# A planned decoder layer: the first two sequences' order, the split of sequences in the front, and the first row scaling

## The chip, the cores and the metric

The kernel runs on one core of a Trainium2 chip. The metric is device time in microseconds (us) of one execution, the median over runs. The profile is one execution of its own; its span runs from the first to the last instruction.

Engine names in the profile: PE is TensorE (matmuls), PEld its weight loads, DVE is VectorE, ACT is ScalarE, POOL is GpSimd, SP is SyncE, which issues nearly all DMAs. A "q" behind a name (SPq, ACTq) marks what an engine's queue issues, DMAs above all.

## The reference

Sixteen sequences of 512 tokens and 256 channels go through one decoder layer in float32, with a layer norm after each of three blocks:

```python
x = _layernorm(x + attn(x))           # long convolution block and a gated MLP
x = _layernorm(x + xattn(x, ctx))     # causal self attention + cross attention, 16 heads of 16
x = _layernorm(x + ffn(x))            # low rank MLP
# attn:  z = rmsnorm(u) @ in_proj.T ; z = short_conv(z) ; x2, x1, v = split(z)
#        xv = x1*v ; y = (long_conv(xv, h) + xv*D_skip) * x2 ; y = y @ out_proj.T + u
#        return y + gelu(rmsnorm(y) @ l1.T) * (rmsnorm(y) @ l2.T) @ l3.T
```

h is a sum of 16 decaying exponentials for each channel. x2 is called the gate below.

## The kernel before

The program has two stages. Each is a list of operations with a cost, a priority (smaller goes first), the tiles that it reads and writes, and the engines that may run it. `Plan.schedule` (L103) places them greedily by these costs, gives every operation a buffer of its class's pool, and emits the instructions in the order found; each engine then runs its own list strictly in order and waits by semaphores. The order is therefore fixed when the program is built, and a wait at the head of an engine's list holds everything behind it.

**The front** (L372 to L987) computes the long convolution of all sequences at once. For each sequence b, `prepare` (L446) loads x, takes the row norms (L319), scales on GpSimd (L333) and transposes (L348). `x1v(b, k)` (L508) projects x1 and v for channel half k (two matmul pairs at L485, short convolution on ACT L492 and DVE L500, product on GpSimd L512), transposes (L518) and copies into `xv[k]`. `gate_of` (L529) projects the two halves of the gate and stores them to DRAM, by SP at L541, or by ACT at L535 for those that are held until after the last matmul of the convolution (`far_done`, L762). The convolution itself is eight blocks, four for each channel half. A block has four Toeplitz tiles of 512 KB ("toes") that SP loads from `hpad` (L669) into the x slots and GpSimd masks (L679), matmuls at L694 (near), L745 (toes) and L757 (far), and four results copied (L301 or L299) and stored to `yconv` (L776).

Three numbers at L432 say how sequences are split in the front. The last LATE sequences do only `x1v(b, 0)` at first, and `x1v(b, 1)` and their gates later, between or beside the blocks. The last KEPT of these hold their normalised x in SBUF (three in the tiles `early`, two in x slots); the other late ones store it to DRAM (`normed`, L557) and load it again (L568). The last LAST sequences project their gates after `far_done`. There are seven x slots, and waiting toes use the same slots.

At the end of the front x, gate and yconv half 0 of sequence 0 are loaded into the three `early` tiles (L792).

**The second stage** (from L1033) runs for each sequence `first_block` (L1107: load y and gate, product L1135, output projection L1148, add L1094, row norm L319/L308/L309, `x_ += y1` on GpSimd L1160, scaling L335, transposes L348, MLP L1173, L1203, L1225, layer norm L1046/L1067), `attention` (L1237: transposes L348, projections L1326 and L1254, context keys L1278 and values L1303, score maxima L1421, scores L1543 with exponentials on ACT L1513, sums L1573, cross attention L1601/L1621, output L1083) and `ffn` (L1732). Sequence b's first block is planned beside the attention of sequence b-1, whose waits for ACT it fills. Its output projection waits (`after`) for the list `begun`, the transposes of that attention's input (L1153, L1241); the context matmuls L1278 and L1296 wait for it too. There is one buffer for y, one for the gate, one for y1, and three PSUM buffers `mm`, besides one `scores` (four banks) and one `av`.

`scale_ops` (L327) scales the four row groups of a tile; for y1 all four run on ACT (L1163).

Of the kernel before, what the change touches and what calls it, by code (L numbers as in the profile page):

```python
# [197 lines left out]
def decoder_layer(  # L198
# [39 lines left out]
    B, T, D = x.shape  # L238
# [46 lines left out]
    def dve(n):  # L285
        return 0.16 + n / 960.0

    def act(n, bias=False):
        return 0.18 + n / 1200.0 + (0.12 if bias else 0.0)

    def pool_(n):
        return 0.2 + n / 470.0
# [20 lines left out]
    def rms_ops(x, prio):  # L313

        sq, junk = Buf("small"), Buf("junk")
        for c in range(NT):
            plan.op(
                "ACT", act(D) + 0.2,
                lambda e, c=c: nc.scalar.activation(  # L319
                    junk.t, x.t[:, c, :], AF.Square, accum_out=sq.t[:, c, 0:1]  # L320
                ),
                prio, r=[(x, c)], w=[(sq, c), junk],
            )
        rsqrt_op(sq, 0, 1.0 / D, 1e-6, prio)
        return sq

    def scale_ops(x, sq, prio, on):  # L327
        for c in range(NT):

            def fn(e, c=c):  # L330
                if e != "ACT":
                    eng = nc.vector if e == "DVE" else nc.gpsimd
                    eng.tensor_scalar(x.t[:, c, :], x.t[:, c, :], sq.t[:, c, 8:9], None, ALU.mult)  # L333
                else:
                    nc.scalar.activation(x.t[:, c, :], x.t[:, c, :], AF.Copy, scale=sq.t[:, c, 8:9])  # L335

            cost = {"POOL": pool_(D), "DVE": dve(D), "ACT": act(D, True)}[on]
            plan.op(on, cost, fn, prio, r=[sq], w=[(x, c)])

    def transposed(src, view, prio, dst=None):  # L340

        dst = dst or Buf("xT")
        for k in range(KD):
            ps = Buf("mm")

            def tr(e, k=k, ps=ps):
                for c in range(NT):
                    nc.tensor.transpose(ps.t[:, bass.ts(c, P)], view(src.t)[:, c, bass.ts(k, P)], ident)  # L348

            plan.op("PE", TR, tr, prio, r=[src], w=[ps])  # L350
            plan.op(
                "ACT DVE", (act(T), dve(T)), lambda e, k=k, ps=ps: copy(e, dst.t[:, k, :], ps.t), prio,
                r=[ps], w=[(dst, k)],
            )
        return dst
# [16 lines left out]
    with ExitStack() as front:  # L372
# [56 lines left out]
        marks = []  # L429


        LATE, KEPT, LAST = 9, 5, 2  # L432

        def at_step(n):
            return marks[n : n + 1] if n >= 0 else ()
# [6 lines left out]
        def as_xT(b):  # L442
            n = b - (B - KEPT)
            return View(f"e{n}" if 0 <= n < 3 else "x", lambda t: t.rearrange("p (k n) -> p k n", k=KD))

        def prepare(b, pr):  # L446

            x_ = View("x", lambda t: t.rearrange("p (c d) -> p c d", c=NT))
            for c in range(0, NT, 1 if b == 0 else NT):
                cs = slice(c, c + (1 if b == 0 else NT))  # L450
                plan.op(
                    "SP", 0.5 if b == 0 else 0.5 * MB,
                    lambda e, cs=cs: nc.sync.dma_start(
                        out=x_.t[:, cs, :], in_=x[b].rearrange("(c p) d -> p c d", p=P)[:, cs, :]
                    ),
                    pr - 1000, w=[(x_, c)] if b == 0 else [x_], lat=2.5, after=at_step(b - 3),
                )
            if b == 0:
                load_in(prew, pre_w, -900, [(INW, "p")])
                for k in range(KD):  # L460
                    load_in(inw[:, k, :], in_wT[bass.ts(k, P), :], -900, [(INW, k)])
                load_in(cw, conv_w, -890, [(CW, 0)])
                load_in(cb, conv_b, -890, [(CW, 1)])
                for k in range(KD):
                    plan.op(
                        "DVE", 0.9,
                        lambda e, k=k: nc.vector.tensor_scalar(
                            inw[:, k, :], inw[:, k, :], prew[:, k : k + 1], None, ALU.mult
                        ),
                        -900, r=[(INW, "p")], w=[(INW, k)],  # L470
                    )

            sq = rms_ops(x_, pr - 120)
            scale_ops(x_, sq, pr - 120, "POOL" if b else "DVE")
            xT = transposed(x_, lambda t: t, pr - 120, as_xT(b))
            marks.append(plan.ops[-1])
            return xT
# [69 lines left out]
        for b in range(B):  # L547
            xT = prepare(b, b * 100)
# [4 lines left out]
            else:  # L553
                if b < B - KEPT:
                    plan.op(
                        "SP", 0.5 * MB,
                        lambda e, b=b, xT=xT: nc.sync.dma_start(  # L557
                            out=normed[b - B + LATE], in_=xT.t.rearrange("p k n -> p (k n)")
                        ),
# [3 lines left out]
        for b, xT in late:  # L563
            if b < B - KEPT:
                xT = as_xT(b)
                plan.op(
                    "SP", 0.5 * MB,
                    lambda e, b=b, xT=xT: nc.sync.dma_start(  # L568
                        out=xT.t.rearrange("p k n -> p (k n)"), in_=normed[b - B + LATE]
                    ),  # L570
# [85 lines left out]
        for blk in range(NR // R8):  # L656
# [106 lines left out]
            for c in range(HPG):  # L763
# [8 lines left out]
                for par in range(2):  # L772
# [9 lines left out]
                    o = plan.op("ACT" if par and blk >= NR // R8 - 3 else "SP", 0.6, store, pc + 10, r=[res], lat=3.0)  # L782
# [318 lines left out]
    def add_row(x, row, prio):  # L1101
        def fn(e):
            nc.gpsimd.tensor_tensor(x.t, x.t, row.unsqueeze(1).to_broadcast([P, NT, D]), ALU.add)

        plan.op("POOL", pool_(NT * D), fn, prio, w=[x])

    def first_block(b, after):  # L1107

        p0, p1, p2 = (b - 2) * 1000 + 300, (b - 1) * 1000 + 100, (b - 1) * 1000 + 150
# [30 lines left out]
        y1 = Buf("y1")  # L1140
# [14 lines left out]
        sq = rms_ops(y1, p0)  # L1155
        for cp in range(NT // 2):
# [3 lines left out]
                lambda e, sl=sl: nc.gpsimd.tensor_tensor(x_.t[:, sl, :], x_.t[:, sl, :], y1.t[:, sl, :], ALU.add),  # L1160
                p0, r=[(y1, 2 * cp), (y1, 2 * cp + 1), sq], w=[(x_, 2 * cp), (x_, 2 * cp + 1)],
            )
        scale_ops(y1, sq, p0, "ACT")  # L1163
        zT = transposed(y1, lambda t: t, p0)
        gT = Buf("gT")
        for f in range(NF):
# [70 lines left out]
    def attention(b, x_):  # L1237

        p0, p1, p3 = (b - 1) * 1000 + 600, b * 1000, (b + 1) * 1000 + 250
        xT = transposed(x_, lambda t: t, p0)  # L1240
        begun = [o for _, o, w in xT.seen if w]  # L1241
        add_row(x_, bias_p, p0 + 100)
        va, vc, yT = Buf("va"), Buf("vc"), Buf("xT")
        keys = [Buf("keys") for _ in range(G)]
# [27 lines left out]
        if b % 2 == 0:  # L1272
# [3 lines left out]
            def kc_mm(e, ps=ps):  # L1276
# [13 lines left out]
                p0, r=[ps], w=[kcs_of[-1]],  # L1290
# [523 lines left out]
    begun, held, kcs_of = (), [], []  # L1814
    for b in range(B):
        x_ = first_block(b, begun)
        begun = attention(b, x_)
        ffn(b, x_)
# [98 lines left out]
```

## Time and profile before

| what | value |
|---|---|
| median of 3 runs | 2086.71 us (2084.34, 2086.71, 2374.48) |
| the profiled execution: its own time | 2084.24 us |
| its span | 2082.2 us |
| what lies around the span | 2.0 us |
| PE busy | 2006.2 us, 96% of the span |
| DVE, ACT, POOL busy | 1329.4, 1029.3, 766.9 us |
| first matmul of the convolution blocks (L694) | 172.75 us |
| last matmul of the convolution (L757) ends | 264.2 us |
| first output projection (L1148) | 281.56 us |
| first transposes of the first attention (L348) | 333.24 us |
| first score maxima of the first and second attention (L1421) | 358.24 and 452.97 us |

In the timeline each row has the start, the busy time of a merged group, engine, line, operation, output and input, the number of instructions, and in brackets the idle time of the engine just before, with what ended it. In the table by windows the columns are the window, its length, busy time and number of instructions for each engine, then the granted PE clock (1.00 is full), the DMA engines' share and GB/s. A float32 matmul shows as two PE records.

### The profile page before, as it was taken

Reading aid. Unit: us, or ns where it says so; the run is one execution under the profiler, and the core shown is the slowest. Engines: PE = TensorE matmul, PEld = TensorE weight load, DVE = VectorE, ACT = ScalarE, POOL = GpSimd, SP = SyncE. Lnnn points to the kernel's source line nnn. Section 1 sums busy time; section 2 is a strip of 40 time slices with the busy share of each in tenths; the row PEclk is TensorE's granted clock in tenths of the full one; section 3 lists DMA queues with packets and bytes.
Section 4 is the critical chain, followed back from the end, with each engine's and each line's share of the span. In section 5 each row is a group of like instructions: output and inputs, shape, how many; then the busy total and the mean of one; then the engine's idle time right before and its main releaser. Section 6 shows DMA issues by size and latency. Waiting matters only on the chain. (4 is left out here: it accounts for less than half of the span.)

```text
span 2082.2 us, 36835 instructions
## 1 busy us (share of the span) xinstructions
PE 2006.2 (96%) x14900; PEld 1053.5 (51%) x14900; DVE 1329.4 (64%) x1920; ACT 1029.3 (49%) x1465; POOL 766.9 (37%) x1036
## 2 busy tenths in 40 slices
PE   7999978999999999999999999999999999999987
PEld 4455645555554545454545454454545454545443
DVE  7987533737584848484857576666767584656554
ACT  6864422656435262717161626253534446655773
POOL 7695612243323241414142424232323233533432
PEclk9999989999999999999999999999999999999999
DMA  6365861030304040413131312223131404031200
GB/s 195 110 212 184 273 214 51 6 119 17 119 11 144 12 134 22 123 33 117 38 108 48 100 56 88 68 70 85 56 100 33 123 13 129 18 101 45 71 22 31
DMA packets 114939, 182.22 MB, mean 88 GB/s; under 512 B 13393, under 2 KB 62034, under 8 KB 114642
## 3 DMA queue, kind: packets, MB, share of 16 engines
q1 hardware_dynamic: 113234, 177.26, 27.8%
q8 instruction: 117, 1.92, 0.4%
q10 hardware_dynamic: 1536, 2.62, 0.4%
q14 instruction: 52, 0.43, 0.1%
HBM read 111.09 MB, written 68.76 MB: 86 GB/s over the span
## 5 line engine op out<-in xcount | busy, mean ns | idle before, releaser
L1513 ACT ACTIVATE ex<-scores 128x2048 f32<-128x2048 f32 (+1 forms) x228 | 362.4, 1606 | 193.5 <-PE scores L1543 140.6
L1173 PE MATMUL mm<-xT,w_l 128*128 128x512 f32 x640 | 299.7, 609 | 0.0
L1560 POOL TENSOR_SCALAR_AFFINE_SELECT ex<-ex 128x512 f32<-128x512 f32 x256 | 158.6, 634 | 324.7 <-ACT ex L1513 323.2
L1421 PE MATMUL scores<-keys,q 32*128 32x192 f32 (+5 forms) x2848 | 225.3, 426 | 6.2 <-ACT ex L1444 4.6
L1543 PE MATMUL scores<-q,keys 32*128 32x256 f32 (+3 forms) x2240 | 183.3, 435 | 11.8 <-ACT ex L1513 10.9
L1421 PEld LDWEIGHTS scores<-keys,q 32*128 32x128 f32 x2848 | 123.8, 184 | 138.5 <-issue 41.1
L1772 ACT ACTIVATE row<-mm,b_s 128x512 f32<-128x512 f32 x124 | 78.9, 686 | 224.7 <-PE mm L1764 224.0
L1173 PEld LDWEIGHTS mm<-xT,w_l 128*128 128x128 f32 x640 | 114.6, 190 | 141.5 <-issue 134.3
L1703 POOL TENSOR_TENSOR nd<-nd,nd 128x1024 f32<-128x1024 f32 x30 | 70.7, 2357 | 299.9 <-DMA nd<-di 299.9
L1573 PE MATMUL av<-ex,va 128*32 128x512 f32 (+3 forms) x2048 | 164.8, 438 | 0.8 <-POOL ex L1560 0.8
L1225 PE MATMUL mm<-w_l,gT 128*128 128x256 f32 x640 | 160.7, 386 | 0.0
L308 POOL TENSOR_SCALAR small<-small 128x4 f32<-128x4 f32 (+1 forms) x66 | 13.2, 200 | 399.7 <-DVE small L1047 359.6
L500 DVE SCALAR_TENSOR_TENSOR frow<-fmm,cw,frow 128x511 f32<-128x511 f32 x192 | 141.0, 744 | 25.9 <-ACT frow L492 21.1
L1470 DVE TENSOR_TENSOR scores<-scores,mask_qk 128x1024 f32<-128x1024 f32 x132 | 115.6, 876 | 60.4 <-PE scores L1421 57.4
L1185 ACT ACTIVATE row<-mm 128x512 f32<-128x512 f32 x80 | 47.8, 598 | 209.6 <-PE mm L1173 209.6
L1543 PEld LDWEIGHTS scores<-q,keys 32*128 32x128 f32 x2240 | 96.9, 184 | 107.5 <-ACT ex L1513 67.3
L1444 ACT COPY ex<-scores 128x1024 f32<-128x1024 f32 (+1 forms) x96 | 114.3, 1228 | 65.7 <-PE scores L1421 53.0
L485 PE MATMUL fmm<-fx,inw 128*128 128x512 f32 x312 | 143.4, 604 | 0.0
L1225 PEld LDWEIGHTS mm<-w_l,gT 128*128 128x128 f32 x640 | 117.2, 190 | 44.6 <-issue 31.1
L299 DVE COPY row<-av 128x512 f32<-128x512 f32 x60 | 41.5, 691 | 134.9 <-PE av L1573 124.4
L1326 PE MATMUL mm<-xT,wqc_s 128*128 128x512 f32 x256 | 126.3, 611 | 0.0
L1332 DVE TENSOR_SCALAR q<-mm,bqc_s 128x512 f32<-128x512 f32 x62 | 46.6, 751 | 100.0 <-PE mm L1326 100.0
(210 smaller groups left out, 3485.9 us busy)
## 6 DMA issues: line engine op xcount, KB each, us to landing
dn<-row SPq DMA_DIRECT2D x120, 256.0 KB
keys<-dk SPq DMA_DIRECT2D x64, 256.0 KB
nd<-dn SPq DMA_DIRECT2D x30, 512.0 KB
nd<-di SPq DMA_DIRECT2D x30, 512.0 KB
fx<-hpad SPq DMA_DIRECT2D x28, 512.0 KB
early<-gates SPq DMA_DIRECT2D x16, 512.0 KB
early<-yconv SPq DMA_DIRECT2D x32, 256.0 KB
dk<-row SPq DMA_DIRECT2D x32, 256.0 KB
```

The lines of the kernel that those rows point to most:

```text
L485: nc.tensor.matmul(ps.t, inw[:, k, bass.ts(m, P)], xT.t[:, k, :], start=(k == 0), stop=(k == KD - 1))
L500: lambda e, lag=lag: nc.vector.scalar_tensor_tensor(t.t[:, lag:], ps.t[:, 0 : T - lag], cw[:, m, 2 - lag : 3 - lag], t.t[:, lag:], ALU.mul ...
L1173: nc.tensor.matmul(ps.t, w[:, k, bass.ts(f, P)], zT.t[:, k, :], start=(k == 0), stop=(k == KD - 1))
L1225: nc.tensor.matmul(ps.t[:, bass.ts(cc, D)], gT.t[:, f, bass.ts(c, P)] if f < NF else gE.t, w_l3[:, f, :] if f < NF else w_l3e[:, c, :], st ...
L1326: nc.tensor.matmul(ps.t, w[:, k, cols], xT.t[:, k, :], start=(k == 0), stop=(k == KD - 1))
L1421: nc.tensor.matmul(sc.t[:, r, lo:hi], q.t[hd, bass.ts(i, P)], kk.t[hd, k0 - at + lo : k0 - at + hi], start=True, stop=True,)
L1444: lambda e, sc=sc, both=both, cols=cols: nc.scalar.copy(both.t[:, :, cols], sc.t[:, :, cols]),
L1470: nc.vector.tensor_tensor(diag, diag, mask, ALU.add)
L1513: lambda e: nc.scalar.activation(ex.t.rearrange("p (r n) -> p r n", r=HPG)[:, :, cols], sc.t[:, :, cols], AF.Exp, scale=scale),
L1543: nc.tensor.matmul(sc.t[:, r, lo:hi], keys[g].t[hd, TC + j * P : TC + (j + 1) * P], qas[g].t[hd, q0 + lo : q0 + hi], start=True, stop=True,)
L1560: lambda e, ex=ex, at=at: nc.gpsimd.affine_select(out=ex.t.rearrange("p (r n) -> p r n", r=HPG)[:, :, at : at + P], in_=ex.t.rearrange("p ...
L1573: nc.tensor.matmul(av[g].t[bass.ts(r, SLOT), j * P :], va.t[:, j, h * VS : h * VS + SLOT], ex.t[:, r * T + at : r * T + at + n], start=(j ...
```

## The change

Three edits. `LATE` goes from 9 to 7 and `LAST` from 2 to 1: sequences 7 and 8 are done whole at once, only 9 and 10 go by DRAM (before, 7 to 10), and only sequence 15 projects its gate after `far_done` (before, 14 and 15). `begun` is empty for sequences 0 and 1, so that the first blocks of sequences 1 and 2 and the context matmuls of sequences 0 and 1 are no longer held until the transposes of attention 0 or 1. The scaling of y1 for sequence 0 may go to ACT or DVE, as the planner finds them free.

```diff
-            cost = {"POOL": pool_(D), "DVE": dve(D), "ACT": act(D, True)}[on]
+            cost = tuple({"POOL": pool_(D), "DVE": dve(D), "ACT": act(D, True)}[o] for o in on.split())
             plan.op(on, cost, fn, prio, r=[sq], w=[(x, c)])
...
-        LATE, KEPT, LAST = 9, 5, 2
+        LATE, KEPT, LAST = 7, 5, 1
...
-        scale_ops(y1, sq, p0, "ACT")
+        scale_ops(y1, sq, p0, "ACT" if b else "ACT DVE")
...
         xT = transposed(x_, lambda t: t, p0)
-        begun = [o for _, o, w in xT.seen if w]
+
+        begun = [o for _, o, w in xT.seen if w] if b > 1 else []
```

What the planner makes of it, read from the two built programs (an order, without times; L numbers from here on are those of the kernel before). The first 38 groups of PE's list are the same; from there on the front is interleaved anew. Between `far_done` and the first L1148, PE's list before holds 14 gate matmuls (L485); after it holds 10, then the context matmuls L1278 (four) and L1303 (two), moved up from the first attention. After the transposes of y1 of sequence 0 one matmul of sequence 1's output projection stands; the other seven stand behind ten of L1225, all in the PSUM buffer that L1203 uses next. After the MLP of sequence 0 come the transposes of sequence 1's y1, one L1148 of sequence 2 and eight of the 20 matmuls L1173 of sequence 1's MLP, and only then the transposes of attention 0. On DVE both products L1135 now stand behind all ten L500 of the last gates, the eviction L1286 of the context keys and two copies of the values (L299). On SP the stores and loads of `normed` go from four of each to two of each, the gate stores L541 from 28 to 30, and ACT's L535 from four to two. SP's list is the same from its 192nd group on, and PE's, DVE's, ACT's and POOL's lists fall back into the same long runs from the fourth sequence or so on, with other buffer numbers.

## The prediction

> **What bounds the kernel now.** I read the page first, then PE's waits by stretch, then PE's timeline at the seam between the stages.
>
> ```profile
> PE 2006.2 (96%) x14900; PEld 1053.5 (51%) x14900; DVE 1329.4 (64%) x1920; ACT 1029.3 (49%) x1465; POOL 766.9 (37%) x1036
> ...
> PE   7999978999999999999999999999999999999987
> ```
>
> PE is busy 96% of the span, so time can be won only where PE idles or runs slowed. The slices that fall short are the start, the seam (slices 6 and 7 of 52 us) and the tail. The change touches neither start nor tail; the seam is what it can reach. PE's waits from 264 to 340 us:
>
> ```profile
> PE mm L1148 <- DVE early L1135: 5.9, 2, 5.2
> PE mm L348 <- ACT y L335: 5.5, 2, 5.1
> PE mm L348 <- ACT early L1067: 4.9, 3, 4.6
> PE mm L1225 <- DVE gE L1216: 0.7, 1, 0.7
> ```
>
> 17.0 us of idle: waiting for the last loads, for the norm of y1, and for the layer norm of sequence 0. The timeline shows what follows a wait:
>
> ```profile
> 281.56 2.04 PE L1148 MATMUL mm<-outw,early 128*128 128x256 f32 x4 [5.19 <-DVE early L1135]
> 284.33 5.49 PE L1148 MATMUL mm<-outw,early 128*128 128x256 f32 x12 [0.72 <-DVE early L1135]
> ...
> 333.24 0.33 PE L348 MATMUL mm<-ident,early 128*128 128x128 f32 x1 [4.60 <-ACT early L1067]
> 333.73 0.33 PE L348 MATMUL mm<-ident,early 128*128 128x128 f32 x1 [0.16 <-ACT early L1067]
> 334.23 1.82 PE L348 MATMUL mm<-ident,early 128*128 128x128 f32 x6 [0.16 <-ACT early L1067]
> 335.98 2.08 PE L1326 MATMUL mm<-xT,wk_s 128*128 128x512 f32 x2
> 337.84 5.13 PE L1148 MATMUL mm<-outw,early 128*128 128x256 f32 x16
> ```
>
> Here L1148 takes 0.32 to 0.46 us a record; later, without a wait, ten records of L1225 of the same size take 2.32 us (0.23). The table by windows says why (clock in the column after POOL):
>
> ```profile
> 104.00:108.00 4.00, 4.00 (x12) 1.83 (x11) 3.27 (x7) 2.40 (x7) 1.27 (x1) 0.83 0.80 259
> 282.00:286.00 4.00, 3.28 (x8) 2.10 (x8) 3.16 (x6) 0.78 (x1) 0.00 (x0) 0.50 0.96 285
> 302.00:310.00 8.00, 8.00 (x20) 3.57 (x19) 1.86 (x3) 1.19 (x2) 0.00 (x0) 1.00 0.00 0
> 88.00:172.75 84.75, 79.11 (x274) 41.52 (x272) 73.51 (x113) 52.37 (x116) 60.40 (x61) 0.96 0.54 164
> 172.75:264.16 91.41, 85.76 (x1642) 59.51 (x1641) 50.89 (x71) 36.32 (x86) 52.94 (x69) 0.98 0.83 264
> ```
>
> After a 5 us wait the clock is half; a wait costs its length and again some us of slow matmuls. The last two rows are the front's part with a new order: before the convolution blocks PE idles 5.6 us and loses 0.04 x 84.75 = 3.4 us of clock, 9.0 together; in the blocks 5.6 + 0.02 x 91.41 = 7.5, with DMA at 0.83.
>
> **The change part by part.** The sum stands against the profiled execution, 2084.24 us (span 2082.2 plus 2.0), which is 2.5 below the median of the runs. Matmul work is conserved; only idle and slow time count.
>
> *a. The seam until the first L1148.* PE passes `far_done` at 264.16 and starts L1148 at 281.56. That start is set by stores and loads: yconv's last stores, and the load L1113 that SP issues at 278.08, behind gate stores L541. In the new order four gate matmuls fewer lie in these 17.4 us (4 x 0.86 = 3.4 us, now ahead of `far_done`), and the context matmuls move in: L1278 0.9 and two L1303 of 0.45. Idle grows by 3.4 - 1.8 = +1.6. SP still has three gate stores made after `far_done` ahead of L1113, so its issue stays where it is.
>
> *b. A new wait.* L1278 writes the PSUM bank of the last gate of sequence 15, so it waits for the tenth L500 on DVE; before, nine end at 277.45, so the tenth ends near 278.2. Its eviction L1286 on DVE writes SBUF that this gate's row held, and so waits until ACT's last L535 has landed. Behind it on DVE are the value copies and both L1135, for which L1148 waits. Landings here: L792 issued at 276.12 is used at 280.77, L1113 issued at 278.08 at 283.58, so 4.7 and 5.5 us; a gate store L541 issued at 262.12 frees its row at 263.87, 1.7 us. L535 at 278.4 lands at 280.1 to 283.9; then 0.69 + 2 x 0.30 + 0.69 on DVE gives the first L1135 at 282.1 to 285.9 instead of 281.46, with both halves ready at once, where now the second comes at 284.27. Cost 0 to +5; I take +2, nearer the short end, since the store goes by ACT's queue beside SP's loads.
>
> By the Trainium skill, "DMA: Bandwidth & Descriptors", Anatomy of one DMA, the fixed cost of a transfer is about 2 us; by that this term would be near 0, by the 4.7 and 5.5 us here it is +3. By "TensorE: Matmul & The Clock Gate", Part 1, the clock falls only after an idle window of about 3.4 us and recovers after 3.4 us busy; the context matmuls then could leave L1148 warm, worth another 7.5 - 3.5 = 4.0 us. The 0.83 after an idle of only 1.98 us at 99.4 speaks against that, and no gain is taken.
>
> *c. The hole at 328.6.* It held 4.60 + 0.32 us idle and slow work after it: L348 2.5 instead of 0.9, L1148 5.1 instead of 3.5 and 0.2 on L1326, 3.3 together. The new order puts the transposes of sequence 1's y1 (0.9), L1148 (0.4) and eight L1173 (6.9) there, 8.2 us, more than the hole is long. What they need is early: sequence 1's L1148 ends some 4 us after L1225's first ten; its norm chain takes as long as that of sequence 0 (289.8 to 297.8, 8 us), while PE has 8 us of L1203 and L1225. Gain -8.2. Against it, seven L1148 and L1203 share one PSUM buffer and twice wait for an L1094 (0.69 and two handoffs, 0.85): +1.7. Net -6.5, bounds -8.2 (no stall) to -5.0 (sequence 1 late by the new wait on POOL, where two L1135 now stand ahead of the layer norm's L308).
>
> *d. Scaling.* The four L335 run in pairs of 0.91, each pair released by L1160 on POOL; with DVE taking one of a pair, one of 0.46 goes from the path: -0.4 (bounds -0.5 to 0, if the waits on L1160 set it).
>
> *e. Given back.* The fill moved forward lacks later. Attention 0's exponentials come every 3.27 us (413.23 to 416.50) whatever PE adds; groups without fill idle there 0.69, 1.07 and 2.06, mean 1.3. The old order leaves three such groups, the new one three or four, at other places: +1.0 (-1 to +4, if three more lose theirs).
>
> *f. The front before the blocks.* With seven instead of nine sequences that do only `x1v(b, 0)`, each with less PE work for the same row norms and scalings, and four 512 KB transfers of `normed` fewer, the waits there (1.98 on ACT, 1.99 on POOL's L512) should shrink. POOL is busy 48.8 of the 50 us from 110 to 160, and that work stays. I take half of the 9.0, -4.5; bounds -9.0 and +3 (a third more).
>
> *g. The blocks.* Fourteen gate and x1v matmuls more stand before the first L694: of these ten leave the blocks (8.6 us) and with them two transposes (0.9). PE's own work in the stretch falls by 9.5 us, but toes (0.5 MB each, 32 of them) and yconv stores stay, at a DMA share of 0.83, 0.93 to 0.96 late in it. Before the second half's blocks, where PE already idles 2.23 us (236.4), fill between the last L757 of the first half and the next L694 falls from 14 gate and x1v matmuls with two transposes (12.9) to ten with two (9.5). I take +3.5, this loss; bounds 0 (toes come ahead: the x slots are freer) and 13.5 (all 9.5 idle, and 4 more at half clock).
>
> *h. Later.* Orders alike; 0, within 1. Cost of SP's and POOL's other moves: none found on PE's path.
>
> Sum: 1.6 + 2 - 6.5 - 0.4 + 1 - 4.5 + 3.5 = -3.3, so 2084.24 - 3.3 = **2081 us**.
>
> **The rivals.**
>
> *1. Slower: the blocks starve.* Place: L745 waiting for toes from L679. Speaks for it: DMA at 0.93 or more, and the 2.23 us already there. Against: two reloads fewer hold x slots that toes could use, so toes can come ahead. At its price of 13.5 instead of 3.5 the time is 2091; it decides from 6.8 us in this term on, where the sum is zero.
>
> *2. No change: what fills the hole is missed later.* Attentions 0 and 1 are paced by ACT, and their groups idle by what was taken: e at +4.5 instead of +1 gives 2084.5. Against: in the new order projections L1326 move into these groups.
>
> *3. More: front and seam go well.* f at -9.0, b and g at 0: 2081 - 4.5 - 2 - 3.5 = 2071.
>
> *4. The change does nothing:* excluded by the order, in which the hole is filled.
>
> **How the numbers follow.** Forecast 0.50 (2076 to 2086 by its own terms), rival 1 0.20 (2091), rival 2 0.12 (2084.5), rival 3 0.15 (2071), something of over 2% 0.03. The range from 2070 to 2092 reaches to rivals 2, 3 and 1; about 0.09 of rival 1's chance is left out above it, 0.05 of rival 3's below, and the 0.03. 2% is 42 us, about what a measurement of this kernel can tell from no change, and no case reaches it: faster by over 2% 0.01, within 0.96, slower 0.03 (a cost not seen).
>
> **What would show it.** Right: no idle before attention 0's first L348 and a granted clock of 1.00 there; L1286 ahead of L1135 waiting for a gates DMA; L1148's start some 18 to 20 us after the last L757; 10 to 12 us of idle and lost clock between the first L694 and the last L757. Wrong: an idle over 3 us ahead of that L348 (c), over 14 us lost in the blocks (g), L1148 over 22 us after `far_done` (b), or the second attention's first L1421 later than 452.97 (e).

## The result, and the profile after

The changed kernel takes 2093.68 us (median of 6 runs, 2091.77 to 2096.78) where the kernel before took 2086.02 on the same chip (median of 6). The ratio is 1.0041 with a 95% interval of 1.0030 to 1.0051: slower by 8.5 us (6 to 11). That is within 2%, but on the other side of zero from the 2081 that was forecast, and just above its range (2070 to 2092). One run of before, 2374.48 us, was disturbed and is left out of the ratio; without it the median of before is 2085.33. The profiled execution has its own time of 2093.87 us, a span of 2092.2 and a mean granted clock of 0.988 (before 2084.24, 2082.2 and 0.991).

Lines from 1242 on stand one higher in the changed kernel: its L1279 is L1278 of before, L1422 is L1421, L1544 is L1543.

The page of the changed kernel (busy time and share; busy tenths in 40 slices of 52 us):

```profile
PE 2009.3 (96%) x14900; PEld 1057.4 (51%) x14900; DVE 1325.5 (63%) x1915; ACT 1032.8 (49%) x1470; POOL 768.3 (37%) x1036
...
PE   8999869999999999999999999999999999999987
```

The number of matmuls is the same and their busy time 3.1 us longer, so some ran at a lower clock; the span grew by 10.0. PE's waits from 272 to 360 us, the stretch whose waits the forecast listed for before:

```profile
PE mm L348 <- DVE y L333: 6.5, 2, 6.0
PE mm L1279 <- DVE frow L500: 5.4, 1, 5.4
PE mm L1148 <- DVE early L1135: 2.0, 1, 2.0
PE mm L1203 <- DVE y L1094: 0.8, 1, 0.8
PE mm L1148 <- DVE y L1094: 0.8, 1, 0.8
```

The hole of 4.6 us ahead of attention 0 (L348 waiting for ACT's L1067) is gone, as it should be. Two others are there: the context keys L1279 now stand at the head of the seam and wait 5.4 us, and y1's transposes wait for VectorE's L333 longer than they did for ScalarE's L335 (6.5 against 5.5). PE's timeline at the seam:

```profile
286.59 2.05 PE L1279 MATMUL mm<-ctxT,wck_s 128*128 128x128 f32 x8 [5.37 <-DVE frow L500]
288.97 1.78 PE L1304 MATMUL mm<-wcv_s,ctx 128*128 128x256 f32 x4 [0.33 <-POOL ctx L1297]
292.78 5.41 PE L1148 MATMUL mm<-outw,early 128*128 128x256 f32 x16 [2.03 <-DVE early L1135]
304.14 0.69 PE L348 MATMUL mm<-ident,y 128*128 128x128 f32 x2 [5.95 <-DVE y L333]
```

The last L757 ended at 272.45, so L1148 starts 20.3 us after it (before 17.4). Its 16 records take 0.34 us each (0.47 before, 0.23 at full clock): the context matmuls in front have not brought them to full speed.

To see where the 10 us went I set each milestone's time against the matmul work ahead of it in the two orders (matmuls counted in the order of the program, each at the pitch of its form in the traces). At equal work the changed kernel is 4.6 us ahead at the first L694, 4.9 behind at the last L757, 9.3 behind at the first L1148, 7.3 at the first L1173, level (+0.1) at attention 0's first L1421 and first L1543, and 9.7 behind at sequence 2's context keys (L1278, 540.59 us before, 550.24 after). After that nothing more is lost (10.3 at the next L1278 and from there on). So there are two losses, one ahead of L1148 and one in attentions 0 and 1, and one gain, the hole. The second loss is in this table by windows (columns: length, then PE, PEld, DVE, ACT and POOL busy, granted clock, DMA share, GB/s). Rows: attention 0's exponentials, attention 1's maxima, attention 1's exponentials. The kernel before:

```profile
400.06:452.97 52.91, 48.77 (x491) 27.35 (x490) 19.21 (x30) 31.70 (x45) 24.91 (x34) 1.00 0.28 82
452.97:499.20 46.23, 44.16 (x386) 25.63 (x385) 35.26 (x38) 28.98 (x35) 13.12 (x18) 1.00 0.19 60
499.20:540.59 41.39, 41.06 (x472) 24.22 (x471) 18.38 (x34) 30.68 (x43) 17.56 (x30) 1.00 0.21 65
```

The changed kernel:

```profile
409.46:459.49 50.03, 44.66 (x492) 23.33 (x492) 18.78 (x29) 31.39 (x41) 22.20 (x32) 0.97 0.34 97
459.49:502.58 43.09, 38.30 (x333) 21.26 (x332) 33.73 (x35) 26.65 (x31) 15.77 (x19) 0.99 0.17 52
502.58:550.24 47.66, 46.87 (x480) 27.78 (x481) 17.53 (x33) 29.59 (x37) 16.57 (x27) 0.93 0.18 58
```

By the order, PE's work fell by 5.5 us in the first row and by 6.1 in the second, and grew by 2.3 in the third. What left is fill (matmuls that are not the attention's own, here L1148 and L1225 above all); part of the attention's own L1254 moved from the second row into the first. The rows grew shorter by only 2.9 and 3.1 us, and the third became 6.3 us longer with hardly any idle in it, at a clock of 0.93 instead of 1.00. Together 140.5 us before and 140.8 after: 9.4 us of work less, and no time won.

What holds the length of the exponentials is a round trip. There is one `scores` buffer, so PE's next scores L1543 wait until ScalarE has taken the exponentials of the last ones, and ScalarE waits for these scores. ScalarE, then PE's scores, in attention 0 of the kernel before:

```profile
407.97 1.94 ACT L1513 ACTIVATE ex<-scores 128x1024 f32<-128x1024 f32 x2 [1.27 <-PE scores L1543]
411.24 1.94 ACT L1513 ACTIVATE ex<-scores 128x1024 f32<-128x1024 f32 x2 [1.33 <-PE scores L1543]
```

```profile
409.96 1.15 PE L1543 MATMUL scores<-q,keys 32*128 32x256 f32 x16
413.23 1.16 PE L1543 MATMUL scores<-q,keys 32*128 32x256 f32 x24
...
420.81 1.15 PE L1543 MATMUL scores<-q,keys 32*128 32x256 f32 x16
424.01 1.16 PE L1543 MATMUL scores<-q,keys 32*128 32x256 f32 x24 [2.06 <-ACT ex L1513]
```

A turn is 1.15 us of scores, 1.94 of exponentials and the handoffs. With PE full of fill it takes 3.27 us (409.96 to 413.23), and without fill, PE idling 2.06 us, 3.20 (420.81 to 424.01). In the changed kernel there are turns of 3.27 us as well (L1544 at 434.96, 438.23 and 441.50). So work that fits into a turn costs next to nothing, and taking it out wins next to nothing.

PE's timeline between the second and the third row shows where the clock went:

```profile
499.39 1.15 PE L1422 MATMUL scores<-keys,q 32*128 32x256 f32 x16 [2.09 <-ACT ex L1445]
502.58 2.09 PE L1544 MATMUL scores<-q,keys 32*128 32x256 f32 x16 [2.05 <-ACT ex L1445]
504.60 1.22 PE L1225 MATMUL mm<-w_l,gT 128*128 128x256 f32 x2
505.62 1.06 PE L1225 MATMUL mm<-w_l3e,gE 128*128 128x256 f32 x2
```

Two groups without fill wait 2 us each for ScalarE, and the matmuls behind them take twice as long (L1544 x16 2.09 us, later 1.15).

### The profile page after: what moved, and what is told of

It is laid out like the page before. It is cut to its first block, busy times and chain, and to the rows that moved or that the text cites. A ratio compares the mean times of both kernels' runs of the same rounds, so it can differ in the third digit from the quotient of the medians.

```text
span 2092.2 us, 36836 instructions
## 1 busy us (share of the span) xinstructions
PE 2009.3 (96%) x14900; PEld 1057.4 (51%) x14900; DVE 1325.5 (63%) x1915; ACT 1032.8 (49%) x1470; POOL 768.3 (37%) x1036
## 5 line engine op out<-in xcount | busy, mean ns | idle before, releaser
L1173 PE MATMUL mm<-xT,w_l 128*128 128x512 f32 x640 | 299.6, 609 | 0.0
L1422 PE MATMUL scores<-keys,q 32*128 32x192 f32 (+5 forms) x2848 | 225.3, 426 | 5.2 <-ACT ex L1445 4.8
L1544 PE MATMUL scores<-q,keys 32*128 32x256 f32 (+3 forms) x2240 | 185.0, 438 | 16.5 <-ACT ex L1514 12.4
L1422 PEld LDWEIGHTS scores<-keys,q 32*128 32x128 f32 x2848 | 123.8, 184 | 136.2 <-issue 40.8
L1173 PEld LDWEIGHTS mm<-xT,w_l 128*128 128x128 f32 x640 | 115.2, 191 | 142.8 <-issue 135.5
L1225 PE MATMUL mm<-w_l,gT 128*128 128x256 f32 x640 | 161.9, 388 | 0.0
L500 DVE SCALAR_TENSOR_TENSOR frow<-fmm,cw,frow 128x511 f32<-128x511 f32 x192 | 140.8, 744 | 29.8 <-ACT frow L492 25.4
L1544 PEld LDWEIGHTS scores<-q,keys 32*128 32x128 f32 x2240 | 98.0, 186 | 114.3 <-ACT ex L1514 69.7
L485 PE MATMUL fmm<-fx,inw 128*128 128x512 f32 x312 | 141.6, 598 | 1.2 <-DVE frow L500 1.2
L1225 PEld LDWEIGHTS mm<-w_l,gT 128*128 128x128 f32 x640 | 118.2, 191 | 44.2 <-issue 30.6
L299 DVE COPY row<-av 128x512 f32<-128x512 f32 x61 | 42.2, 692 | 141.6 <-PE av L1574 130.5
```

The costliest lines, as they stand in the source:

```text
L485: nc.tensor.matmul(ps.t, inw[:, k, bass.ts(m, P)], xT.t[:, k, :], start=(k == 0), stop=(k == KD - 1))
L500: lambda e, lag=lag: nc.vector.scalar_tensor_tensor(t.t[:, lag:], ps.t[:, 0 : T - lag], cw[:, m, 2 - lag : 3 - lag], t.t[:, lag:], ALU.mul ...
L1173: nc.tensor.matmul(ps.t, w[:, k, bass.ts(f, P)], zT.t[:, k, :], start=(k == 0), stop=(k == KD - 1))
L1225: nc.tensor.matmul(ps.t[:, bass.ts(cc, D)], gT.t[:, f, bass.ts(c, P)] if f < NF else gE.t, w_l3[:, f, :] if f < NF else w_l3e[:, c, :], st ...
L1422: nc.tensor.matmul(sc.t[:, r, lo:hi], q.t[hd, bass.ts(i, P)], kk.t[hd, k0 - at + lo : k0 - at + hi], start=True, stop=True,)
L1544: nc.tensor.matmul(sc.t[:, r, lo:hi], keys[g].t[hd, TC + j * P : TC + (j + 1) * P], qas[g].t[hd, q0 + lo : q0 + hi], start=True, stop=True,)
```

## The experiments

Theory: the filled hole wins nothing in the end, because attentions 0 and 1 hold their length when their fill is taken; what is lost beyond that lies ahead of L1148. Main rival: 7, 5, 1 starves the blocks, which lost 9.5 us at equal work (4.6 + 4.9) between the two first profiles. The three parts alone came first.

| run | edit | us | ratio to before on the same chip, 95% interval |
|---|---|---|---|
| e1 | first two sequences let go | 2086.91 | 1.0008 (0.9994 to 1.0022) |
| e2 | LATE, LAST 7, 1 | 2089.18 | 1.0014 (1.0005 to 1.0023) |
| e3 | scaling on ScalarE and VectorE | 2084.79 | 0.9994 (0.9984 to 1.0004) |
| e4 | LATE, LAST 7, 2 | 2086.62 | 1.0009 (1.0000 to 1.0018) |
| e5 | the changed kernel again | 2090.99 | 1.0028 (1.0012 to 1.0044) |
| e6 | changed, context keys held | 2089.56 | 1.0020 (1.0010 to 1.0030) |
| e7 | changed, without the scaling | 2092.37 | 1.0034 (1.0023 to 1.0046) |
| e8 | four sequences let go | 2118.93 | 1.0159 (1.0139 to 1.0179) |
| e9 | the kernel before again | 2085.59 | 0.9999 (0.9989 to 1.0008) |
| e10 | two let go, context keys held | 2087.94 | 1.0018 (1.0005 to 1.0030) |
| e11 | one let go, context keys held | 2092.42 | 1.0036 (1.0023 to 1.0048) |
| e12 | scaling, and adds on VectorE | 2083.12 | 0.9994 (0.9984 to 1.0004) |
| e13 | before, some fill left out | 2085.41 | 1.0005 (0.9994 to 1.0015) |
| e14 | changed, some fill twice | 2104.45 | 1.0095 (1.0080 to 1.0111) |

Single runs of the kernel before spread from 2079.29 to 2091.14 (35 runs), so one profile stands for its kernel only to some us. The stretches of the profiles, in us, each from the milestone before:

| profile | first L694 | last L757 | L1148 | L1173 | L1421 | L1543 | second L1278 | next L1278 |
|---|---|---|---|---|---|---|---|---|
| before | 172.8 | 91.4 | 17.4 | 16.2 | 60.4 | 41.8 | 140.5 | 195.0 |
| e9 before again | 172.4 | 98.1 | 14.0 | 15.8 | 59.1 | 41.8 | 141.9 | 195.0 |
| changed | 181.0 | 91.4 | 20.3 | 14.8 | 60.4 | 41.4 | 140.8 | 195.7 |
| e5 changed again | 180.6 | 89.8 | 20.6 | 15.8 | 60.4 | 41.4 | 140.8 | 195.5 |
| e1 two let go | 171.3 | 98.4 | 18.1 | 15.3 | 59.8 | 41.4 | 140.8 | 196.8 |
| e2 7, 5, 1 | 181.2 | 89.0 | 16.9 | 13.8 | 60.2 | 41.8 | 141.9 | 195.0 |
| e3 scaling | 171.0 | 100.3 | 14.0 | 15.2 | 60.4 | 41.8 | 142.0 | 195.0 |
| e4 7, 5, 2 | 180.7 | 80.8 | 17.7 | 19.6 | 60.1 | 41.8 | 140.5 | 195.0 |
| e6 keys held | 180.1 | 88.5 | 16.3 | 14.9 | 60.4 | 41.4 | 141.4 | 195.5 |
| e8 four let go | 171.3 | 100.2 | 13.3 | 17.1 | 61.5 | 41.4 | 137.0 | 199.3 |

**e1, the first part alone.**

```diff
-        begun = [o for _, o, w in xT.seen if w]
+        begun = [o for _, o, w in xT.seen if w] if b > 1 else []
```

> The first part of the change alone: the first two sequences hold nothing back; 9, 5, 2 and the scaling stay as before. My theory: the work that fills the hole ahead of attention 0 wins 7 to 9 us up to the first L1421, and all of it is lost again between the first L1543 and sequence 2's L1278, because that stretch keeps its 140.5 us whatever TensorE has to do in it. So the time is that of the kernel before within 2 us: 2085 to 2088, with sequence 2's context keys L1278 at 540 to 542 (before 540.59). Rival (the forecast's own step e): only 1 us is given back, and the time falls by 4 to 6 us, to 2080 to 2082. Second rival: the unheld work costs more later than it wins, 2090 or more, and the other two parts are harmless.

2086.91 us, ratio 1.0008 (0.9994 to 1.0022). At equal work it wins 7.5 us between the first L1173 and the first L1421 and loses 9.7 between the first L1543 and the second L1278: nearly the same two numbers as in the changed kernel (7.2 and 9.6). The forecast's 2080 to 2082 is excluded. The second L1278 came at 545.0, not at 540 to 542, because its blocks took 98.4 us in an order that is that of before; that was the first sign that this stretch isn't fixed.

**e2 and e4, the second part alone, and without its LAST.**

```diff
-        LATE, KEPT, LAST = 9, 5, 2
+        LATE, KEPT, LAST = 7, 5, 1        # e4: 7, 5, 2
```

> The second part alone: 7, 5, 1 for LATE, KEPT, LAST. My theory: the stretch before the first L694 wins 4.6 us net of the moved work, the blocks lose about 9.5, and the seam after the last L757 idles 2 to 4 us more because four gate matmuls fewer lie in it; sum +7 to +9, so 2093 to 2095, and the seam after it is as before (hole of 4.6 us ahead of attention 0). Rival: the blocks lost time only together with the unheld work, and this part alone is within 2 us of before (2084 to 2088).

> LATE 7 and KEPT 5 with LAST at 2 as before: seven late sequences, but one sequence fewer has its gates made in the front's filler. My theory: what the blocks lose is the filler that was moved ahead of them; with LAST 2 the blocks have as many gate matmuls left as with 7, 5, 1 or fewer, so the loss in the blocks stays at 7 to 10 us, and the time is 2092 to 2095. Rival: it is LAST, by the order of the gates, that starves the blocks, and this kernel is within 2 us of before.

e2: 2089.18 us, ratio 1.0014 (1.0005 to 1.0023), that is +2.9 us (1.0 to 4.8): less than half of what the theory expected, and at its lower end within the rival's 2 us. e4: 2086.62, 1.0009 (1.0000 to 1.0018), nearer its rival. Both reach the first L694 some 4 us ahead at equal work (4.4 and 3.7). e4 passes the blocks in 80.8 us, the shortest of all. By these times, fewer late sequences do not cost the blocks 9.5 us.

**e3, the third part alone.**

```diff
-        scale_ops(y1, sq, p0, "ACT")
+        scale_ops(y1, sq, p0, "ACT" if b else "ACT DVE")
```

> The third part alone: sequence 0's row scaling by ScalarE and VectorE, everything else in the order of before. My theory: VectorE's two L333 lie beside POOL's L1160 and L1135 and take 1.3 us each instead of the 0.35 that the same instruction takes at 7 us, so the transposes of y1 start some 0.8 us later than the 294.93 of before; time +0.5 to +1 us (2086.5 to 2087). Rival (as on record): one L335 of 0.46 leaves the path, -0.4 us, and the slow L333 in the changed kernel came from something else in its order.

2084.79 us, ratio 0.9994 (0.9984 to 1.0004): neither sign is shown. Of its two L333 one took 1.33 us and one 0.34. POOL's and VectorE's timelines of this run say when:

```profile
295.87 2.48 POOL L1160 TENSOR_TENSOR early<-early,y 128x512 f32<-128x512 f32 x2
299.63 2.49 POOL L1135 TENSOR_TENSOR early<-early,early 128x512 f32<-128x512 f32 x2 [1.29 <-DMA early<-yconv]
```

```profile
297.16 1.60 DVE L333 TENSOR_SCALAR y<-y,small 128x256 f32<-128x256 f32 x2 [3.83 <-POOL early L1160]
```

The first L333 begins beside POOL's second L1160 (to 298.35) and ends just after it; the second lies in POOL's pause. In the changed kernel POOL goes on to L1135 without a pause, and both are slow (its L333 by form, ns min, median, max):

```profile
L333 DVE TENSOR_SCALAR fx<-fx,fsmall x4: 345/347/353, 7.0 to 9.4; 128x256 f32<-128x256 f32 x4
L333 DVE TENSOR_SCALAR y<-y,small x2: 1334/1344/1353, 302.7 to 304.0; 128x256 f32<-128x256 f32 x2
```

**e5, the changed kernel once more; e9, the kernel before once more.** No edit.

> The changed kernel as it is, for a second profile. What the first four runs showed: kernels whose order up to the last L757 is that of before spent 91.4, 98.4 and 100.3 us from the first L694 to the last L757. Theory: this stretch differs by several us from one execution to the next with the same order, and the 91.4 of before was a short one; here it comes to anything from 84 to 95 us, while the hole (first L1148 to first L1421, 75.2 us) and the stretch from the first L1543 to sequence 2's context keys (140.8) repeat within 1 us. Time 2091 to 2096. Rival: the 91.4 of the changed kernel belongs to its order and repeats within 1 us.

> The kernel before as it is, for a second profile. Six profiles of kernels that share its order up to the last L757, or nearly, took 98.4, 100.3 and 100.2 us (old order) from the first L694 to the last L757, against 91.4 in the profile the forecast was made from. Theory: the 91.4 was a short execution and a second one takes 94 to 101 us, with the first L1173 some 2 to 3 us later than 297.8; the blocks' loss in the forecast (term g) was then mostly a comparison with a lucky profile, since the new order takes 87 to 91 with 9.5 us less work in it. Rival: it repeats 91.4 within 1.5 us and the three edits that do not touch the blocks slowed them.

e5: 2090.99 us, ratio 1.0028 (1.0012 to 1.0044); blocks 89.8, which is 1.6 from the 91.4 and so just outside the rival's 1 us; the stretch to the second L1278 is 140.8 to a tenth. e9: 2085.59, 0.9999 (0.9989 to 1.0008), and its blocks took 6.7 us longer than in the profile that the forecast was made from. The windows from the first L694 to the last L757, e9 first, then the changed kernel:

```profile
172.40:270.51 98.11, 87.70 (x1642) 61.09 (x1641) 52.18 (x73) 36.64 (x86) 53.10 (x68) 0.97 0.81 254
```

```profile
181.04:272.40 91.36, 80.02 (x1614) 57.81 (x1613) 40.84 (x59) 32.60 (x81) 48.03 (x65) 0.93 0.78 251
```

Nine profiles with the old order up to the last L757 took 91.4 to 100.3 us here, mean 96.2; six with that of 7, 5, 1 took 84.9 to 91.4, mean 88.5, with 9.5 us less work in it. At equal work that is a loss of 1.8 us, not of 9.5: the main rival falls. The 91.4 that the forecast read was the shortest of the nine. What makes the stretch differ from one execution to the next wasn't tried.

**e6, the changed kernel with the context keys held.** All three parts are in, but L1278 and the copies L1296 wait as in the kernel before; `free` is what first_block gets.

```diff
         begun = [o for _, o, w in xT.seen if w]
+        free = begun if b > 1 else []
...
-        return begun
+        return free
```

> The changed kernel, but with the context key matmuls and the context copies held as before, so that no L1278 and no L1286 stands in the seam; all else of the change is in. Theory (the forecast's term b): the seam from the last L757 to the first L1148 falls from 20.4 us to 17 to 18.5, and the time by 2 to 3 us against the changed kernel, to 2090 to 2092. Rival: L1148 starts as late as before because its loads are what it waits for, 20 us or more, time 2093 to 2095.

2089.56 us, ratio 1.0020 (1.0010 to 1.0030), 1.4 below e5 in the same series, with intervals that overlap. In the profile the seam is 16.3 us instead of 20.3 and 20.6. What stood there in the changed kernel, from ScalarE's queue, then from POOL, ScalarE and VectorE:

```profile
285.08 1.82 ACTq L535 DMA_DIRECT2D gates<-frow  x2
290.23 0.27 ACT L301 COPY vc<-mm 64x128 f32<-64x128 f32 x1 [6.12 <-DMA gates<-frow]
```

```profile
288.62 0.53 POOL L1297 COPY ctx<-ctxT 128x128 f32<-128x128 f32 x2 [12.18 <-DMA gates<-frow]
```

```profile
290.78 0.69 DVE L1287 TENSOR_TENSOR kcs<-mm,bck_s 128x512 f32<-128x512 f32 x1 [4.33 <-PE mm L1304]
292.04 1.33 DVE L1135 TENSOR_TENSOR early<-early,early 128x512 f32<-128x512 f32 x2
```

The last gate stores L535 are issued from 285.08 on; POOL's context copy and ScalarE's value copy wait for them to land (288.6 and 290.2), L1304 waits for POOL's copy, VectorE's L1287 for L1304, and both L1135 stand behind it. In e5, the second profile of the same program, the wait that the forecast had named is the last to end: VectorE's L1287 itself waits for a gate store.

```profile
289.04 0.69 DVE L1287 TENSOR_TENSOR kcs<-mm,bck_s 128x512 f32<-128x512 f32 x1 [5.54 <-DMA gates<-frow]
290.30 1.33 DVE L1135 TENSOR_TENSOR early<-early,early 128x512 f32<-128x512 f32 x2
```

So it is the wait of the forecast's step b, reached in the first profile by one more engine than it named.

**e7, the changed kernel without its third part** (e3's diff undone).

> The changed kernel without its third part: sequence 0's scaling is on ScalarE alone again. Theory: the transposes of y1 start about 1.2 us earlier after L1148 (wait of 5.1 us on ScalarE's L335 instead of 6.5 on VectorE's L333), and the time falls by 1 us or less, 2092 to 2094: what is lost to the change is in the other two parts together. Rival: the parts alone came to +1.7, +2.9 and -1.3 us, so what is missing to the +8 of the whole lies in how the scaling meets the new order; then this kernel is at 2088 to 2090.

2092.37 us, ratio 1.0034 (1.0023 to 1.0046): the time is in the theory's range, and the rival's 2088 to 2090 is excluded. Y1's transposes wait 5.5 us again, as expected, but no fall of the time is shown: e7 is 1.4 above e5 in the same series, with intervals that overlap. The scaling has no share in the loss that these runs can tell.

**e8, four sequences let go; e11, one.** Both with the context keys held, 9, 5, 2, and ScalarE's scaling.

```diff
         begun = [o for _, o, w in xT.seen if w]
+        free = begun if b > 3 else []        # e11: b > 0
...
-        return begun
+        return free
```

> The first four sequences, not two, let the next sequence's first block go early; context keys and copies held as before; 9, 5, 2 and ScalarE's scaling as before. Theory: attentions 0 and 1 take their time by ScalarE and by waits whatever fill TensorE has, so more fill can only keep them from idling; the work that e1 took from them comes back from sequences 2 and 3, the stretch from the first L1543 to sequence 2's context keys has fewer than 6 us of idle, and the shortage moves to attention 4 and later, where TensorE has work for every wait: the time is 2 to 6 us under before, 2080 to 2084. Rival: the shortage moves along with it and shows up again at attention 4 or at the end, time 2085 to 2088.

> Only sequence 0 lets the next first block go early (sequence 1's); context keys and copies held as before. Theory: what the hole takes is missed in attention 0 alone, and the first block of sequence 2 stays where it was, so attention 1 keeps its fill: the stretch from the first L1543 to sequence 2's context keys (140.5 with all held, 140.8 with two let go) falls to 135 to 139, and the time to 2081 to 2085. Rival: that stretch is set by ScalarE and stays at 140 to 141, time 2085 to 2088.

Both theories fell. e8 takes 2118.93 us, ratio 1.0159 (1.0139 to 1.0179), 33 us more. Attentions 0 and 1 do get their fill back (137.0 us), but the next ones lose theirs: from 541.9 to 960 us PE idles 33.5 us, where before, from 540.6 to 952.6, it idled 2.4. PE's waits from 260 us to the end, e8 and then the kernel before:

```profile
PE scores L1544 <- ACT ex L1514: 32.2, 34, 2.1
```

```profile
PE scores L1543 <- ACT ex L1513: 10.9, 15, 2.1
```

The shortage moves to the next attention and grows on the way. e11 takes 2092.42, ratio 1.0036 (1.0023 to 1.0048): with sequence 2's block held, attentions 0 and 1 are short of fill too, and take 144.5 us (PE idles 10.6 us of it, before 6.5, at a clock of 0.95).

**e10, two sequences let go, keys held** (e6's diff on the kernel before).

> The first part alone with the context keys and copies held as before: only sequences 1 and 2's first blocks are let go early. Theory: no new wait in the seam, so the first L1148 comes 13 to 16 us after the last L757, as in the two runs that held them; the fill of the hole and its loss in attentions 0 and 1 cancel within 2 us; time 2084 to 2088. Rival: without the seam's wait the filled hole is a net gain of 4 us or more, 2079 to 2082.

2087.94 us, ratio 1.0018 (1.0005 to 1.0030): the rival's net gain is excluded. Its seam took 17.2 us, above the 13 to 16 expected. The filled hole, freed of the seam's wait, still wins nothing.

**e12, the scaling with the two adds L1160 moved to VectorE.**

```diff
-                "POOL", pool_(T),
-                lambda e, sl=sl: nc.gpsimd.tensor_tensor(x_.t[:, sl, :], x_.t[:, sl, :], y1.t[:, sl, :], ALU.add),
+                "POOL" if b else "DVE", pool_(T) if b else dve(T),
+                lambda e, sl=sl: (nc.gpsimd if b else nc.vector).tensor_tensor(x_.t[:, sl, :], x_.t[:, sl, :], y1.t[:, sl, :], ALU.add),
```

> The third part alone, with sequence 0's two L1160 adds moved from POOL to VectorE, so that POOL goes straight to its two L1135 (2.5 us) while VectorE runs the two L333. Theory: L333 takes 1.3 us instead of 0.35 whenever POOL works beside it (1.34 and 0.34 in one run, where the second lay after POOL's last L1135 had begun to end), so at least one of the two takes over 1 us, and the gain from the faster adds (0.69 instead of 1.24 each) is eaten: y1's first transposes start 12.5 to 13.5 us after the first L1148, as before (13.4). Rival: L333 is slow because it waits for L1160's own writes; with L1160 on VectorE both take 0.35, and the transposes start 12 us or less after the first L1148.

2083.12 us, ratio 0.9994 (0.9984 to 1.0004). Both L333 took 0.35 us, and the transposes started 11.4 us after the first L1148, as the rival had it. But what my numbers rested on did not come about: POOL's L1135 waited for a load until 294.68, so that POOL was idle beside both L333, and the run does not tell the two readings apart. e3 does: there the slow L333 had waited for L1160 like the fast one behind it, and only POOL's work beside it differed. So does the changed kernel: its second L333, from 304.0 on, runs when both L1160 have ended (303.9), beside L1135, which does not touch y1, and takes 1.33 us or more like the first. The path from the end of L1148 to the first L1173 is 5.8 us here, 8.0 before. This is the lowest median of all, but its interval holds 1, so it isn't shown to beat the kernel before; it beats the changed one.

**e13, fill left out of the kernel before; e14, fill issued twice in the changed one.** Orders and planned costs stay as they are.

```diff
+                        if b == 1 and cp and 0 < f < NF:      # e13, L1225
+                            return
...
+                        if b == 2 and k:                      # e13, L1148
+                            return
...
-                            start=(k == 0), stop=(k == KD - 1),
+                            start=(k == 0), stop=(k == KD - 1 or b == 2),
```

```diff
+                      for again in range(2 if b == 2 else 1):  # e14, L1225
```

> The kernel before, with its order and its planned costs, but most of the fill that the change moved out of attentions 0 and 1 isn't done at all: eight of sequence 1's L1225 and half (four) of sequence 2's L1148 issue nothing, 12 x 0.46 = 5.5 us of matmuls less (so part of the output projection and of the second product of these two sequences is left out). Theory: the stretch from the first L1543 to sequence 2's context keys, 140.5 and 141.9 us in the two profiles of before, is not set by TensorE's work in it; it stays at 139.5 to 142 and the time within 2 us of before. Rival (the forecast's step e): work taken out is time won but for 1 us, so the stretch falls to 135 to 137 and the time by 4 to 5 us.

> The changed kernel, in which sequence 2's L1225 (24 matmuls in attention 1) are issued twice (so its second product is counted twice in part): 24 x 0.46 = 11 us of matmuls more, in the stretch that lost its fill. Theory: there they take the place of idle and of half clock; the stretch from the first L1543 to sequence 2's context keys grows from 140.8 by less than 5 us, its granted clock rises from 0.96 to 0.98 or more, and the time grows by less than 5. Rival: TensorE sets that stretch; it grows by 10 to 11 us and so does the time.

e13: 2085.41 us, ratio 1.0005 (0.9994 to 1.0015). The stretch from the first L1543 to the second L1278:

```profile
399.10:540.10 141.00, 130.95 (x1324) 74.11 (x1324) 72.75 (x102) 91.38 (x121) 55.72 (x81) 0.99 0.22 69
```

141.0 us, between the 140.5 and 141.9 of the kernel before: work that lay for the most part in attention 0's exponentials isn't done at all (4.5 us less busy time than in e9), and not a microsecond came of it; the 4 to 5 us of the rival, the forecast's step e, are excluded. e14: 2104.45 us, ratio 1.0095 (1.0080 to 1.0111), and the same stretch:

```profile
410.90:561.30 150.40, 139.80 (x1352) 81.86 (x1353) 70.11 (x97) 87.66 (x108) 54.53 (x77) 0.97 0.21 65
```

9.6 us longer for 10.0 us more busy time: there my theory fell. The added L1225 stand at places of attention 1 where PE works without a pause, and there work counts in full; the two waits of 2.1 and 2.0 us at the end of its maxima stayed as they were. (Its seam was longer too, 27.1 us after blocks of 84.9; its whole time is no measure of the fill.) So the stretch does have parts in which TensorE sets the time. The fill that the change took lay mostly in those where it does not, and 2.3 us of it went to one where it does.

## Why the prediction was wrong

The terms in us, at equal work; "all profiles" are means over the profiles that share the order of the stretch, or nearly, the changed kernel's less the old one's.

| term | forecast | the two first profiles | all profiles |
|---|---|---|---|
| f, before the blocks | -4.5 | -4.6 | -3.7 |
| g, the blocks | +3.5 | +9.5 | +1.8 |
| a and b, seam to L1148 | +3.6 | +4.4 | +8.7 |
| d, L1148 to L1173, and what else lies there | -0.4 | -2.0 | -0.9 |
| c, the hole | -6.5 | -7.2 | -7.3 |
| e, given back | +1.0 | +9.6 | +9.3 |
| h, later | 0 | +0.6 | +0.6 |
| sum | -3.3 | +10.3 | +8.5 |

Blocks and seam belong together: where the blocks were short the seam was long (e14 84.9 and 27.1 us, e3 100.3 and 14.0). e14 is in both means; without it g is about +2.5 and a and b about +7. Of the 11.8 us between the forecast and the last column, e alone is 8.3.

**Failed: step e, "given back".** It was taken at +1.0 with a bound of +4, and is +8.0 to +11.8 against the first profile of before in the six profiles with two sequences let go and nothing else changed in that stretch (0.9 less against the mean of its kind). The step counted groups without fill and gave each 1.3 us of idle. Two things were left out. First, if the exponentials come every 3.27 us "whatever PE adds", as the step says itself, then all the work that leaves them has to be counted, not only whole groups: 11.6 us left attention 0's exponentials and attention 1's maxima, and those grew shorter by 6.0 only; e13 shows that in attention 0's exponentials such work was free to begin with (taking work out of attention 1's maxima alone was not tried). Second, the clock: of the 140.8 us PE idles 4.4 more than before, and by the clock of the three rows it loses 5.3 more (0.03 x 50 + 0.01 x 43 + 0.07 x 48). The forecast had said that "a wait costs its length and again some us of slow matmuls", and did not apply it here. Rival 2 was this mechanism, at half its price. Its counter-argument, that projections L1326 move in, was true and not enough.

**Step b, the new wait: right in kind, at the far end of its range.** The place, the landing of the last gate stores, was as forecast. In the profiles the first L1148 of the changed order comes some 4 us later than with the keys held (seams of 20.3, 20.6 and, in e7, 22.0 against 16.3 and, in e2, 16.9), forecast +2 of 0 to +5; the times show 1.4 (e6 against e5), which their noise does not set apart from 4. The forecast leaned to the short end for the stores' landing. POOL's copy started 3.5 us after the first of them was issued (288.62 and 285.08), and in e5 VectorE's L1287 over 5 us after the last (289.04 and 283.90): nearer the loads' 4.7 and 5.5 us than the 1.7 of the gate store that the forecast had seen. The 2 us that the forecast quotes from the Trainium skill, "DMA: Bandwidth & Descriptors", Anatomy of one DMA, stand there in a section on transfers that GpSimd issues; these are issued by ScalarE. What is above b in the table comes with a: with 3.4 us of gates fewer behind the last L757, L1148 starts no sooner after it even with the keys held: 16.3 us in e6, where it waits 7.5 us, by the trace for VectorE's last L500, and 16.9 in e2, against 15.5 on the mean of the eight profiles with both the old order and the keys held. SP issues L1113 as late as before, as a had said: 13.9 us after the last L757 before and in e6, 13.7 in the changed kernel.

**Step g, the blocks: right on the mean, and a trap in the first comparison.** Between the two first profiles the blocks seemed to lose 9.5 us, which pointed to rival 1. It was the profile of before that was short there, by 5 us against the mean of nine. The forecast's own sign for rival 1, over 14 us lost in the blocks, did show: 11.3 us of idle and 0.07 x 91.4 of clock, 17.7 together. But the sign was set by the short profile; e3, in the old order, lost 16.4 us there. Rival 1 did not come about.

**Steps f and c: right**, f at -3.7 to -4.6 and c at -7.2: no idle ahead of attention 0's first L348, and a clock of 1.00 there.

**Step d: too small to matter, with the wrong sign in the changed kernel's own path.** One L335 did leave it, but each L333 took 1.34 instead of 0.35 us beside POOL, and the wait of y1's transposes grew by 1.0 (5.5 to 6.5). The -2.0 in the table comes from L1148, whose two halves were ready at once, as b had said. The Trainium skill, "Advanced Engine Details and Errata", VectorE Performance Modes, says that VectorE's second SBUF port is shared with GpSimd, and that GpSimd's instructions and VectorE's two-port ones block each other; the 1.33 and 0.34 us of e3, with and without POOL beside it, agree with that, though no run here shows the port itself, or that L333 is a two-port instruction. The forecast had not looked at what POOL does beside the instruction that it moved.

**The clock gate.** The forecast had weighed the idle window of some 3.4 us in the Trainium skill's "TensorE: Matmul & The Clock Gate" (Part 1) against the trace and taken no gain for L1148. That was nearly right: its 16 records took 5.4 us instead of 7.5 at a granted clock of 0.68, and not the 3.5 of full clock; they took 6.3 in e5 and, with no context matmuls ahead of them, 6.2 in e6. On the fall of the clock the runs differ from the page: two waits of 2.09 and 2.05 us, 1.15 us of matmuls between them, were followed by half clock from 502.58 on (granted 0.50 until 507).

## What to carry to other kernels

Fill that is moved forward into a hole is won only if the stretch that it leaves gets shorter by it: look there first at what sets its pace. Where that is not this engine's own work (here it was a round trip of two engines over one buffer), the fill was free, its place stays idle, and the idle can cost clock on top. A chain of such stretches passes the shortage on, so holding work back can be the better order. And one profile is one execution: before a difference of a few us is laid on a change, profile the kernel before a second time.

## What was not expected of the hardware

A VectorE instruction of 0.35 us took 1.33 beside GpSimd's work, and 0.34 in GpSimd's pause, in the same run (e3). The same program's convolution blocks, at a DMA share of 0.81 to 0.83, took 91.4 and 98.1 us in two executions of the kernel before, while the stretch from the second L1278 to the next, which moves little data (DMA share 0.22), took 195.0 both times.
